# When the first inverse transform of a strip is placed: a planner's condition on VectorE's clock

## The chip, the cores and the metric

The kernel runs on one core of a Trainium2 chip. A core has TensorE (PE in the profile; its weight loads are shown apart as PEld), VectorE (DVE), ScalarE (ACT), GpSimd (POOL) and SyncE (SP, which here only issues transfers). Each engine works through its own list of instructions in order, and semaphores make it wait for other engines. The metric is the device time of one execution in microseconds (us), lower is better.

## The reference, cut to what matters

Four layers, each `x = x + layer(group_norm(x))`, on a float32 tensor of 4 images, 48 channels, 256 x 256 pixels. Only layer 0 is touched by the change:

```python
h = jnp.einsum('bchw,oc->bohw', x, w_in)                  # 48 -> 192 channels
h = jax.lax.conv_general_dilated(h, w_dw, ..., feature_group_count=2 * HID)   # 3x3, channel by channel
x1, x2 = jnp.split(h, 2, axis=1)
h = jax.nn.gelu(x1, approximate=False) * x2
y = jnp.einsum('bchw,oc->bohw', h, w_out)                 # 96 -> 48 channels
yp = y.reshape(b, c, Hp // P, P, Wp // P, P).transpose(0, 1, 2, 4, 3, 5)      # 8x8 blocks
f = jnp.fft.rfft2(yp.astype(jnp.float32)) * fft_w         # a mask on the block's spectrum
yp = jnp.fft.irfft2(f, s=(P, P))
```

Layers 1 and 2 are recurrent scans over rows and columns with small convolutions; layer 3 is like layer 0 with more channels and the transform in another place.

## The kernel before, in words

Layer 0 works through 64 strips, each of 8 rows of two images. For one strip n, the steps and their lines are these.

- `hidden` and `hidden_rest` (lines 278 to 296) make the 192 hidden channels by matmuls into PSUM tiles `ph`; ScalarE copies them into `main` (128 of the channels) and `rest` (64).
- Two generators `lane(0)` and `lane(1)` (line 300) do the 3x3 convolution of the main channels on TensorE: nine taps, each of 8 matmuls by a diagonal matrix (line 313), into a PSUM tile `pd`; one `yield` after each tap. Lane 0 ends in a gelu on ScalarE (`gl`, line 324), lane 1 in a product on VectorE (`g`, line 327). A lane waits at the start of an image until the strip's main half is `ready`.
- `unit` (line 334) does the convolution of the rest channels on VectorE, 16 instructions of line 352 a strip (`acc`), each about 1.3 us.
- `mixed` (lines 384 to 409) does the matmul back to 48 channels (`py`, lines 392 and 399) and a copy to `y`; `turned` (line 411) transposes it (`pt`, `yt`); `waves` (line 425) does the forward transform (`pf`, line 434), and VectorE multiplies with the mask in two instructions (`z`, line 438), one for each half.
- `back` (line 445) brings the strip back to pixels, in two pieces: `back(n, z, 0)` and `back(n, z, 8)`. Each does 32 matmuls (64 records in the profile) into a PSUM tile `po` (line 462), and eight additions of the input on VectorE (`xo`, line 473). The first piece reads the first half of `z` alone. The first issues the loads of `res` on SP (line 451); the second adds the statistics (line 482) and issues the stores on POOL (line 485).

All PSUM tiles of layer 0 share one pool, `ps`, with four buffers; a new tile waits until the engine that read the buffer's last tile is done.

The order is not left to a scheduler: `by_clocks` (line 565) writes it, while the program is built, with two planned clocks. `self.pe` is TensorE's: each step of a lane adds 0.54. `self.dve` is VectorE's. In each round both lanes take one step. Then pieces of `work()` (line 493) are placed, in their order. A piece is four things: a condition, a planned PE time, what it does, and a planned DVE time. It is placed when the credit that the lanes' steps have earned is not negative, when its condition holds, and, if it has a DVE time, when `self.dve` is less than 1.5 ahead of `self.pe`; its PE time is then taken from the credit, which grows to 2.0 at most. Lastly `due` (line 604) places VectorE's taps, as long as `self.dve` is not more than 1.0 ahead of `self.pe`. Placing the piece of `waves` moves `self.dve` by its planned 2.2 (`after`, line 600), so that right after it `self.dve` stands for the planned end of the mask. The condition of the first piece of `back` is `always`.

Of the kernel before, what the change touches and what calls it, by code (L numbers as in the profile page):

```python
# [33 lines left out]
class Net:  # L34
# [133 lines left out]
    def layer0(self, scs, stats):  # L168
# [7 lines left out]
        with ExitStack() as st:  # L176
# [11 lines left out]
            for half in range(2):  # L188
                lo = half * HID0
                for b in range(2):  # L190
                    s = slice(64 * b, 64 * b + C)
                    nc.sync.dma_start(wi[s, 64 * half : 64 * half + 64], self.a["L0_w_in"][:, lo : lo + 64])
                    at = 64 * half + 32 * b
# [16 lines left out]
            for j in range(4):  # L210
                s = slice(32 * j, 32 * j + 32)
                nc.sync.dma_start(wo[s, :, 0:C], self.a["L0_w_out"][0:64, :].rearrange("(k c) o -> c k o", c=32))
                at = 64 * (j % 2)
# [53 lines left out]
            def halo(n):  # L267
                h0 = strips[n][1]
                for z in (mains, rests):
                    new, old = z[n % 2], z[1 - n % 2]  # L270
                    if h0 == 0:
                        nc.gpsimd.memset(new[:, :, 0, 1 : W + 1], 0.0)
                    else:
                        nc.gpsimd.tensor_copy(new[:, :, 0:2, 1 : W + 1], old[:, :, RB : RB + 2, 1 : W + 1])
                    if h0 + RB == H:
                        nc.gpsimd.memset(new[:, :, RB + 1, 1 : W + 1], 0.0)
# [10 lines left out]
            def hidden_rest(n, xn, chunks):  # L287
                ph = sums("ph")
                for i, (r0, r1) in enumerate(chunks):
                    nc.tensor.matmul(  # L290
                        ph[:, i, 0 : r1 - r0, :], wi_r[0:112, :], xn[0:112, r0:r1, :], start=True, stop=True
                    )
                if all(r1 - r0 == R2 for r0, r1 in chunks):
                    chunks, ph = [(chunks[0][0], chunks[-1][1])], ph.rearrange("p i r w -> p (i r) w").unsqueeze(1)
                for i, (r0, r1) in enumerate(chunks):
                    nc.scalar.copy(rests[n % 2][:, 0, r0 + 1 : r1 + 1, 1 : W + 1], ph[:, i, 0 : r1 - r0, :])
# [148 lines left out]
            def back(n, z, q0):  # L445


                p, h0 = strips[n]
                res = sums_of[n % 2]
                for b in range(2 if q0 == 0 else 0):  # L450
                    nc.sync.dma_start(res[64 * b : 64 * b + C], self.x0[p, b * C : (b + 1) * C, h0 : h0 + RB, :])
                if q0 == 0:
                    state["xo"] = io.tile([CP, 2, self.WB, 2, RH, 2, 8], F32, name="xo", tag="xo")
                xo = state["xo"]
                for q0 in (q0,):
                    po = ps.tile([128, 2, 4, 2, 2, RH, 2, 4], F32, name="po", tag="w")
                    for q in range(4):
                        for l in range(2):
                            for lo, m in ((0, 64), (64, C)):
                                for o in range(2):  # L460
                                    f = slice(64 * o, 64 * o + 64)
                                    nc.tensor.matmul(
                                        po[lo : lo + m, o, q, :, :, :, l, :].rearrange("p e f h w -> p (e f h) w"),
                                        z[f, q0 // 2 + q, l, lo : lo + m], self.inv1_p[f, :],
                                        start=True, stop=True,
                                    )
                    rs = res[:, :, q0 * PW : (q0 + 8) * PW].rearrange(
                        "p (h e) (q w f) -> p e f q h w", e=2, f=2, q=8
                    )
                    for e in range(2):  # L470
                        for f in range(2):
                            for o in range(2):
                                nc.vector.tensor_tensor(
                                    xo[:, e, q0 // 2 : q0 // 2 + 4, f, :, o],
                                    po[0:CP, o, :, e, f].rearrange("p q h l w -> p q h (l w)"),
                                    rs[:, e, f, o::2], ALU.add,
                                )
                if q0 + 8 < NQ:
                    return
                flat = xo.rearrange("p e v f h l w -> p (e v f h l w)")  # L480
                for k in range(RB * W // MM):
                    nc.vector.bn_stats(stats[p][:, h0 * W // MM + k, :], flat[:, k * MM : (k + 1) * MM])
                to = self.strip(self.xs[0], p, h0 // 2, h0 // 2 + RH)
                for b in range(2):
                    nc.gpsimd.dma_start(
                        to[b].rearrange("c e v h w -> c (e v) (h w)"),
                        xo[64 * b : 64 * b + C].rearrange("p e v f h l w -> p (e v f) (h l w)"),
                    )

            ready, taken, state = set(), {}, {}  # L490
            full, until = {}, {}

            def work():


                always = lambda: True

                def enter(n):
                    return (lambda: n < 2 or taken.get(n - 2, 0) == 6), 0.0, lambda: halo(n), 0.0

                def fill(n, rest):
                    for k in range(0, 6 if strips[n][1] == 0 else 4, 2):
                        def go(k=k):
                            xn, chunks = state["xn"]
                            if rest:
                                hidden_rest(n, xn, chunks[k : k + 2])
                            else:
                                for r0, r1 in chunks[k : k + 2]:
                                    hidden(n, xn, r0, r1)
                            if k + 2 >= len(chunks):  # L510
                                ready.add((n, int(rest)))
                                if rest:
                                    full[n] = self.pe + 4.0
                        yield always, 1.8, go, 0.0

                early = self.norm_steps([stats[0]], self.grp7, "e", lambda name: sums(name)[0:CP, 0, 0, 0:1])

                parts_of = [1, 2, 2, 1]

                def advance():  # L520
                    try:
                        for _ in range(parts_of.pop(0)):
                            next(early)
                    except StopIteration as end:
                        state["first"] = self.by_image(0, end.value[0], nc.sync)

                fetch(0)
                fetch(1)
                state["xn"] = normed(0)
                yield enter(0)  # L530
                yield from fill(0, True)
                yield from fill(0, False)
                state["xn"] = normed(1)
                for n in range(len(strips) + 1):
                    if n == 4:
                        for which in ("down", "right", "left"):
                            self.scan_weights(1, which)
                    if n + 2 < len(strips):
                        fetch(n + 2)
                    if n > len(strips) // self.NP and "first" not in state:  # L540
                        yield always, 0.2, advance, 0.0
                    if n:
                        yield (
                            lambda: taken.get(n - 1, 0) == 6 and self.pe >= until[n - 1], 4.0,
                            lambda: state.update(y=mixed(n - 1)), 0.0,
                        )
                    if n + 1 < len(strips):
                        yield enter(n + 1)
                        yield from fill(n + 1, True)
                    if n:  # L550
                        yield always, 1.8, lambda: state.update(yt=turned(state["y"])), 0.0
                    if n + 1 < len(strips):
                        yield from fill(n + 1, False)
                    if n:
                        yield always, 1.7, lambda: state.update(z=waves(state["yt"])), 2.2
                    if n + 2 < len(strips):
                        state["xn"] = normed(n + 2)
                    if n:
                        yield always, 2.0, lambda: back(n - 1, state["z"], 0), 1.7
                        yield always, 1.1, lambda: back(n - 1, state["z"], 8), 4.4  # L560

            self.by_clocks([lane(0), lane(1)], work(), 0.54, [unit(n) for n in range(len(strips))])
            return state["first"]

# [1032 lines left out]
```

## Time and profile before

| | us |
|---|---|
| time before, median of 3 runs | 12764.71 (12756.09 to 12771.58) |
| the profiled execution | 12765.85 |
| its span, first to last instruction | 12764.0 |
| PE busy in the span | 11837.9 |
| DVE busy in the span | 7893.1 |
| ACT busy in the span | 4689.4 |

Layer 0's taps start at 259.4 us, and its last piece of `po` at 2968.5 us, so layer 0 is about a fifth of the span.

In a line of the profile that tells waits, "PE po L462 <- DVE z L438: 30.4, 26, 3.1" means that TensorE, ahead of an instruction of line 462 that writes `po`, waited for the instruction of line 438 on VectorE that writes `z`: 30.4 us in all, 26 times, 3.1 us the longest. "issue" is idle time in which the engine waited for nothing that the profile shows. In a line in order of time come the start, the duration, the engine, line, operation, tiles, shapes and the number of records; in brackets stands the idle time before it and who ended it. A float32 matmul shows as two records.

### The profile page before, as it was taken

The page shows a single profiled execution, that of the slowest core. Times are in us where ns is not written, and L with a number is a line of the kernel's source. Part 1 is how long each engine was busy: PE and PEld are TensorE (multiplying, and loading weights), DVE is VectorE, ACT ScalarE, POOL GpSimd, SP SyncE. Part 2 cuts the span into 40 slices and gives each one's busy share as a digit, 9 for nine tenths or more (in the row PEclk, how much of TensorE's full clock was granted, in tenths as well). Part 3 has the DMA queues.
Part 4 walks back from the last instruction along what each step waited for, and adds up shares of the span by engine and source line. Part 5 has one row for each costly group of instructions (what it writes and reads, how often), then busy time and mean ns, then how long its engine had stood idle before and what let it go on. Part 6 is the DMA issues. An engine that isn't in the chain of part 4 may idle for free. (4 is left out here: it accounts for less than half of the span.)

```text
span 12764.0 us, 411497 instructions
## 1 busy us (share of the span) xinstructions
PE 11837.9 (93%) x190576; PEld 7844.3 (61%) x190576; DVE 7893.1 (62%) x11132; ACT 4689.4 (37%) x5761; POOL 3135.4 (25%) x2017
## 2 busy tenths in 40 slices
PE   2999999999999999999999999989999999989998
PEld 1333333336777777777777777766666666666665
DVE  6777777774333334663333335668888777777787
ACT  1444444442223200002233000036666666666665
POOL 0000010000000001540000004534444444444344
PEclk9999999999999999999999999999999999999999
DMA  7222222226765876988756977931111111111110
GB/s 178 57 59 57 59 54 62 59 54 110 151 138 148 177 152 137 225 200 157 146 141 154 175 150 172 229 83 28 28 28 28 28 21 31 28 23 28 28 28 21
DMA packets 1170307, 1223.68 MB, mean 96 GB/s; under 512 B 1027668, under 2 KB 1031756, under 8 KB 1107724
## 3 DMA queue, kind: packets, MB, share of 16 engines
q1 hardware_dynamic: 1066052, 623.85, 26.6%
q0 software_dynamic: 87488, 445.55, 12.2%
q10 hardware_dynamic: 15048, 127.96, 5.4%
q8 instruction: 1494, 24.48, 0.8%
q14 instruction: 225, 1.84, 0.1%
HBM read 699.79 MB, written 497.42 MB: 94 GB/s over the span
## 5 line engine op out<-in xcount | busy, mean ns | idle before, releaser
L689 PE MATMUL acc<-line,w_down 96*96 96x256 f32 x12240 | 2660.9, 379 | 14.6 <-ACT line L787 4.9
L1269 POOL TENSOR_TENSOR acc_m<-acc_m,part 128x512 f32<-128x512 f32 (+1 forms) x1040 | 1820.0, 1771 | 2445.1 <-ACT part L1268 2423.7
L689 PEld LDWEIGHTS acc<-line,w_down 96*96 96x96 f32 x12240 | 1989.1, 163 | 671.7 <-DVE line L831 11.5
L1242 DVE SCALAR_TENSOR_TENSOR acc<-z_b,wd,acc 128x1024 f32<-128x1024 f32 (+1 forms) x1056 | 1818.3, 1722 | 40.9 <-ACT acc L1237 11.8
L313 PE MATMUL pd<-main,diag 32*32 32x512 f32 x36864 | 1401.8, 612 | 94.3 <-issue 54.9
L689 PE MATMUL acc<-line,w_right 96*96 96x256 f32 x6120 | 1339.6, 379 | 27.3 <-DVE line L869 22.1
L352 DVE SCALAR_TENSOR_TENSOR acc<-rest,wd,acc 128x1024 f32<-128x1024 f32 x1024 | 1275.2, 1303 | 145.0 <-ACT acc L344 144.8
L1178 PE MATMUL pd<-z_a,diag 32*32 32x512 f32 x37152 | 1317.7, 596 | 48.3 <-issue 43.2
L689 PE MATMUL acc<-line,w_left 96*96 96x256 f32 x6120 | 1336.6, 379 | 9.9 <-DVE line L910 7.5
L689 PEld LDWEIGHTS acc<-line,w_right 96*96 96x96 f32 x6120 | 997.0, 163 | 358.2 <-DVE line L869 22.9
L689 PEld LDWEIGHTS acc<-line,w_left 96*96 96x96 f32 x6120 | 994.7, 163 | 338.5 <-DVE line L910 16.4
L1178 PEld LDWEIGHTS pd<-z_a,diag 32*32 32x32 f32 x37152 | 793.9, 103 | 474.3 <-issue 196.3
L124 ACT ACTIVATE nrm<-nrm 96x2 f32<-96x2 f32 (+1 forms) x7 | 1.4, 203 | 2798.2 <-DVE nrm L123 2768.4
L872 DVE SCALAR_TENSOR_TENSOR line<-acc,b_right,in 96x256 f32<-96x256 f32 x1020 | 489.4, 480 | 850.7 <-PE acc L689 848.2
L796 DVE TENSOR_TENSOR line<-acc,in 96x256 f32<-96x256 f32 x1020 | 429.1, 421 | 920.0 <-PE acc L689 914.1
L831 DVE SCALAR_TENSOR_TENSOR line<-acc,b_down,in 96x256 f32<-96x256 f32 x992 | 476.0, 480 | 830.5 <-PE acc L689 821.9
L313 PEld LDWEIGHTS pd<-main,diag 32*32 32x32 f32 x36864 | 494.4, 104 | 780.2 <-issue 670.6
L1103 DVE TENSOR_TENSOR z<-pz,mask 128x768 f32<-128x768 f32 (+2 forms) x640 | 629.3, 1006 | 509.1 <-PE pz L1100 506.5
L920 POOL TENSOR_TENSOR blk<-blk,line 96x1024 f32<-96x1024 f32 x248 | 705.0, 2872 | 607.1 <-DVE line L910 607.1
L838 ACT COPY blk<-line 96x1024 f32<-96x1024 f32 (+2 forms) x264 | 480.0, 1891 | 921.8 <-DVE line L831 759.4
L910 DVE SCALAR_TENSOR_TENSOR line<-acc,b_left,in 96x256 f32<-96x256 f32 x992 | 475.6, 479 | 528.3 <-PE acc L689 528.3
L1268 ACT ACTIVATE part<-z_m,none,wd 128x512 f32<-128x512 f32 (+1 forms) x1040 | 786.1, 803 | 7.2 <-POOL acc_m L1269 7.1
(167 smaller groups left out, 13626.9 us busy)
## 6 DMA issues: line engine op xcount, KB each, us to landing
blk<-x ACTq DMA_DIRECT2D x64, 1536.0 KB, 17.5
in<-x SPq DMA_DIRECT2D x248, 384.0 KB, 11.1
dn<-line POOLq DMA_DIRECT2D x124, 768.0 KB, 9.8
rt<-line POOLq DMA_DIRECT2D x124, 768.0 KB, 9.9
in<-rt SPq DMA_DIRECT2D x124, 768.0 KB, 11.5
in<-dn SPq DMA_DIRECT2D x120, 768.0 KB, 6.5
in<-up SPq DMA_DIRECT2D x240, 384.0 KB, 11.5
up<-blk POOLq DMA_DIRECT2D x56, 1536.0 KB, 14.3
```

What stands on the lines that cost most here:

```text
L313: nc.tensor.matmul(pd[32 * j : 32 * j + 32, i], diag[s, t, :], z[s, R2 * j + t // 3 : R2 * j + t // 3 + R2, t % 3 : t % 3 + W], start=(t = ...
L352: nc.vector.scalar_tensor_tensor(to, at(t, r), wd[:, 1, t : t + 1], to, ALU.mult, ALU.add)
L689: self.nc.tensor.matmul(acc, w[:, t, :], carry[:, :, t : t + m], start=(t == 0), stop=(t == 2))
L831: nc.vector.scalar_tensor_tensor(inner(line), acc, bd, new[r], ALU.add, ALU.add)
L838: nc.scalar.copy(blk[:, :, e, lo:hi, k // 2 : k // 2 + RH], inner(ln[:, e::2])[..., lo:hi].rearrange("p h i w -> p i w h"),)
L872: nc.vector.scalar_tensor_tensor(blocks(inner(line)), blocks(acc), br, new, ALU.add, ALU.add)
L920: (nc.vector if w0 == 0 else nc.gpsimd).tensor_tensor(part, part, inner(ln[:, f::2])[..., lo:hi].rearrange("p w i h -> p i h w"), ALU.add)
L1103: nc.vector.tensor_tensor(zs[k][:, q0 : q0 + n].rearrange("p q b c -> p b q c"), pz[:, :, :, 0:NM], mask[:, :, :, NM * k : NM * k + NM].to ...
L1178: nc.tensor.matmul(pd[32 * j : 32 * j + 32, i, 0:n, :], diag[s, half, t, :], zt[g][s, R2 * j + t // 3 : R2 * j + t // 3 + n, t % 3 : t % 3 ...
L1242: nc.vector.scalar_tensor_tensor(acc, at(t), wd[:, half, t : t + 1], acc, ALU.mult, ALU.add)
L1268: nc.scalar.activation(part, half(at(t), r), AF.Identity, bias=none[0:n], scale=wd[0:n, 2, t : t + 1])
L1269: nc.gpsimd.tensor_tensor(half(acc, r), half(acc, r), part, ALU.add)
```

## The change

The first piece of `back` has a condition of its own. When it is first asked, it notes VectorE's planned time; the piece is placed only when TensorE's planned time has reached it. Before each strip's piece the noted time is cleared. The second piece keeps its condition.

```diff
                 always = lambda: True
+
+                def masked():
+                    if "at" not in state:
+                        state["at"] = self.dve
+                    return self.pe >= state["at"]
 
                 def enter(n):
...
                     if n:
-                        yield always, 2.0, lambda: back(n - 1, state["z"], 0), 1.7
+                        state.pop("at", None)
+                        yield masked, 2.0, lambda: back(n - 1, state["z"], 0), 1.7
                         yield always, 1.1, lambda: back(n - 1, state["z"], 8), 4.4
```

The condition is asked only when the credit isn't negative, and between `waves` and that moment `due` may have placed taps on VectorE, which also move its planned time.

## The prediction

> **What bounds the kernel now.** I read the page's head first: one core, and TensorE (PE) is busy almost throughout.
>
> ```profile
> span 12764.0 us, 411497 instructions
> PE 11837.9 (93%) x190576; PEld 7844.3 (61%) x190576; DVE 7893.1 (62%) x11132; ACT 4689.4 (37%) x5761; POOL 3135.4 (25%) x2017
> ```
>
> The change touches only layer 0, whose taps (`pd`, line 313) run from 259 us to about 2971 us. Over that stretch the windows give PE 2512 us of 2713 busy, VectorE (DVE) 2057, ScalarE (ACT) 1200: PE sets the pace and idles about 200 us. So the next view is the list of PE's own waits in that stretch (who it waited for, total, times, longest):
>
> ```profile
> PE pd L313 <- issue: 54.9, 35, 3.1
> PE po L462 <- issue: 35.1, 21, 3.4
> PE po L462 <- DVE z L438: 30.4, 26, 3.1
> PE ph L282 <- ACT main L285: 21.2, 21, 1.0
> PE pd L313 <- DVE z L438: 17.8, 11, 1.7
> PE pd L313 <- ACT gl L324: 17.8, 15, 2.1
> ```
>
> The product with the mask (`z`, line 438) holds PE up in two ways, which the change treats differently: 30.4 us at `po` (line 462), the piece that is moved, and 17.8 us at a new `pd`, which can't have its PSUM buffer before `z` has read `pf`. That 48.2 us is all there is to win by waiting more cleverly for the mask: 0.38%. A larger figure, 82.6 us of `po` weight loads waiting for `z`, should not be used; the weight-load row shows 0.84 us of idle at such places even when the matmul row shows none.
>
> Two strips in order of time show the two ways. First one where `po` waits:
>
> ```profile
> 1018.32 1.74 PE L434 MATMUL pf<-yt,c_fwd 64*64 64x448 f32 x16
> 1019.98 1.16 PE L313 MATMUL pd<-main,diag 32*32 32x512 f32 x32
> 1021.78 2.07 DVE L438 TENSOR_TENSOR z<-pf,mask 128x896 f32<-128x896 f32 x2
> 1022.91 1.15 PE L462 MATMUL po<-c_inv_p,z 64*64 64x64 f32 x64 [1.77 <-DVE z L438]
> 1024.14 1.68 DVE L473 TENSOR_TENSOR xo<-po,res 112x128 f32<-112x128 f32 x8 [0.29 <-PE po L462]
> ```
>
> `pf` ends at 1019.98, one round of taps (both lanes, 32 records) takes 1.09 us, and PE then stands 1.77 us: the first half of `z` (1.075 us of the 2.07) started late, behind taps of VectorE. `z`'s first half is thus ready about 2.85 us after `pf`, its second some 1.07 later. In the next strip the stall is at a new `pd`, and `po` behind it waits for nothing:
>
> ```profile
> 1060.87 1.16 PE L313 MATMUL pd<-main,diag 32*32 32x512 f32 x32
> 1063.66 1.15 PE L313 MATMUL pd<-main,diag 32*32 32x512 f32 x32 [1.63 <-DVE z L438]
> 1064.75 1.15 PE L462 MATMUL po<-c_inv_p,z 64*64 64x64 f32 x64
> ```
>
> **The change, part by part.** No instruction is added or removed; the order by clocks gives other positions. Comparing the order of instructions built from both codes:
>
> (a) *`po` comes one round later* in nearly every strip: after two or three rounds behind `pf` instead of one or two. Where it stalled 1.77 us, 1.77 - 1.09 = 0.68 us remains. In strips 0 to 29 the pattern repeats every five strips. Before, one cycle (strips 24 to 28) has 0.97 + 0.73, 0, 1.77, 1.63 and 0 = 5.1 us of waits for gelu and mask between `pf` and `po`. After: one strip with a new `pd` half a round later (1.63 - 0.54 = 1.09) and four with at most 0.68 = 3.8. Gain 1.3 us a cycle, six cycles: -8 us.
>
> (b) *What a saved stall gives back.* The rows "issue" total 92 us, waits for nothing the profile shows. They cut single pieces apart, such as this `po`, 9 records and then 55:
>
> ```profile
> 1617.85 0.38 PE L462 MATMUL po<-c_inv_p,z 64*64 64x64 f32 x9
> 1621.31 1.03 PE L462 MATMUL po<-c_inv_p,z 64*64 64x64 f32 x55 [3.08 <-issue]
> ```
>
> The Trainium skill ("Runtime: NRT & Kernel Launch", Instruction fetch mechanics) says that instructions stream in blocks of 256 and that this is mostly hidden, since issue is slower than the fetch. By that rule the -8 us is kept whole. The row speaks against it: a `po` is 64 matmuls and 64 weight loads in 1.08 us, and between `pf` and `py` the strips with a 1.65 or 1.77 us stall (11, 16, 21, 26, 38, 43, 48, 53, 58) have 0.9 us of issue gaps on average, those without one (13, 18, 23, 28, 40, 45, 50, 55, 60) have 2.4 us. That the gaps are fetching is not shown, but a stall there seems to be spent twice. The groups differ in their number of taps too, so I take half: +4 us, ends 0 and +8.
>
> (c) *The two tap lanes fall into step.* This the diff doesn't show. Before, lane 1 runs some rounds behind lane 0 in every strip, so `pd` tiles end one at a time. In the changed order lane 0 is held two steps near strip 30 (its main half isn't there yet), lane 1 catches up, and from strip 31 to the end both `pd` end and begin in the same round. PSUM has four such buffers (`ps`, 4), so two must come free at once, twice a strip.
> Between `pf` and `py`, per cycle of five (41 to 45): one strip where both new `pd` follow `pf` by one round and wait for both halves of `z` (1.66 + 0.5), two where `po` waits 0.68, one where two `po` are followed a round later by two new `pd` that wait for `xo` (eight adds, 1.68 us a `po`: 0.3 + 1.2), one with 0.3. Together 5.4 us against 5.1: +2 us over six and a half cycles.
> In mid-strip, where before almost nothing waits, there are three forms. 13 strips: a `ph` just before, whose copy ends 0.1 + 1.01 us after it while the first `pd` covers 0.54: 0.6 us. 8 strips: the gelu (1.03 us) is nearly covered: 0.2. 11 strips: both new `pd` follow `pt`, whose two copies take 1.71 us (0.15 + 0.5), and the second `ph` then waits for the gate product (1.03 gelu, then 1.215 us product, up to one 1.3 us tap before it: 0 to 0.7): 1.0. Sum 7.8 + 1.6 + 11 = +20 us; ends 0 (the copies come earlier than I place them) and +45 (a VectorE tap ahead of every product).
> The skill ("Perfetto Trace Analysis", Optimization Strategy) says that a gap that repeats on the saturated engine can mean that there isn't enough PSUM for the next tile. It would charge more for this than the rows do: an unhidden gelu and product, 2.2 us, at each of 65 joint ends is 145 us. I take the rows, since the two free buffers cover most of it.
>
> (d) *VectorE does one or two more taps between `z` and `xo`* (1.28 us each), and while `po` 0 waits the order saves up credit, so in 26 strips `po` 8 follows at once. Two buffers are then held until two sets of adds (3.4 us) are done. Five of the 26 are in (c). In the others the next new tile comes two rounds later (2.2 us) or one; I take 0.6 us for each of 21: +12 us, ends 0 and 1.7 x 21 = 36.
> The output DMA waits for `xo` on POOL, and the next `res` load on SP: both move by one tap, 1.3 us. POOL's wait for `xo` is already 707 us, and `res` is needed a strip (42 us) later; landing takes 6 to 8 us. Nothing for these, and 1.3 us a strip if that slack were gone.
> ACT has 1513 us idle in the stretch; its moved gelus count only as in (c). Behind a waiting `po` or `pd` all PE work of the strip queues, and then `y`, `rest` and `main` on ACT: they go late by the stall itself, not again.
>
> Sum: -8 + 4 + 2 + 20 + 12 = +30 us on the profiled execution's 12765.85 us (span 12764.0 and 1.85 around it): 12795.9. The median of the runs is 1.1 us under the profiled one: **12794 us**, +0.23%. What measurement of this kernel can tell from no change is about 0.2%, 25.5 us.
>
> **The rivals.**
> *Hidden or given back.* The issue gaps swallow (a) whole, and the staggered first half shows that two free buffers suffice: (c) and (d) bring 5 us or so. Time about 12768. For it: one cycle of five strips takes 206 us (975.32 to 1181.70) and the one ahead of it (758.05 to 975.32) 217 us before the change, with the same order, so gaps of this kind move more time than the mask does. Against it: (c) is a lasting change of structure in 33 strips.
> *Faster.* The mask's 48.2 us and part of the gelu's 17.8 go, and joint ends are free because ACT is idle over half the time. Less the remainders of 0.68 in some 30 strips (20 us): -45, about 12720 to 12735. It decides if joint ends cost less than 0.5 us a strip and gaps give nothing back. Against it: 11 of the 37 mask waits stand at `pd`, where moving `po` does nothing.
> *Much slower.* Every pair of adjoining `po` holds two of four buffers through a late set of adds, 1.68 us and more in 26 strips, and every joint end pays a tap in front of the product: +36 and +45 on top of (a): about +75, 12840. For it: the adds follow one tap more than before. Against it: `py` waits for `xo` only 2.0 us in all now.
> *Nothing happens* is excluded: the built order differs in nearly every strip.
>
> **How the numbers follow.** The forecast (own range 12765 to 12830) has 0.50, hidden 0.17, faster 0.21, much slower 0.12. The range leaves out the outer part of faster and of much slower, a tenth at each side: 12733 to 12847. Slower by over 0.2% (above 12790.2): 0.6 of the forecast and all of much slower = 0.42. Within 0.2%: the rest of the forecast and nearly all of hidden, 0.36. Faster: 0.22.
>
> **What would show it.** In the list of PE's waits after the change: `po` for `z` down from 30.4 to under 20 us (a); issue rows over 92 us (b); new rows of `pd` for `rest`, `yt`, `gl`, `z` and `xo` after about 1610 us, and the stretch from there to layer 0's end longer than the 1361 us of before while the first half is no longer (c); `pd` or `py` waiting for `xo` well over 2.0 us (d). The rest of the kernel should keep its length. I am wrong if lanes in step cost PE nothing, or if PE's waits fall and the time with them.

## The result, and the profile after

The changed kernel takes 12789.27 us (median of 17 runs, 12768.46 to 12827.14), the kernel before 12773.54 us in the same comparison (17 runs, 12756.09 to 12797.55). The ratio is 1.0014, with a 95% interval of 1.0007 to 1.0020: slower by some 18 us, clear of noise, and smaller than the 0.2% (25.5 us) that the prediction gave as what measurement can tell from no change. The forecast was 12794 us, 1.0023.

The head of the page of the changed kernel: TensorE (PE) has the same instructions and 20 us more busy time.

```profile
span 12784.7 us, 411481 instructions
PE 11858.4 (93%) x190576; PEld 7860.0 (61%) x190576; DVE 7877.3 (62%) x11132; ACT 4692.7 (37%) x5761; POOL 3166.9 (25%) x2017
```

From the list of PE's own waits in layer 0 of the changed kernel, the rows that bear on the parts of the prediction:

```profile
PE po L462 <- issue: 41.6, 22, 3.8
PE pd L313 <- issue: 39.6, 27, 3.1
PE pd L313 <- ACT gl L324: 21.9, 14, 2.1
PE pd L313 <- DVE z L438: 15.0, 12, 1.9
PE po L462 <- DVE z L438: 12.8, 11, 1.9
PE ph L282 <- ACT gl L324: 11.7, 11, 1.2
PE po L462 <- DVE xo L473: 3.4, 8, 0.4
PE pd L313 <- ACT yt L420: 2.5, 11, 0.2
PE py L392 <- DVE xo L473: 2.0, 5, 0.6
```

The condition did what it says: `po` waits 12.8 us for the mask instead of 30.4, and a new `pd` 15.0 instead of 17.8. The row of `ph` for `gl` grew from one wait to eleven, each a little over one microsecond. Two windows of 30 strips show where the time is: strips 0 to 29 (first `pf` to the `pf` of strip 30), then 30 to 59. First the kernel before, then the changed one; the columns are the length and the busy time of PE, its weight loads, DVE, ACT and POOL, then the granted clock, the DMA share and the GB/s that the DMA engines moved.

```profile
321.00:1609.80 1288.80, 1190.01 (x24075) 483.72 (x24070) 967.69 (x1266) 563.88 (x546) 117.46 (x122) 0.97 0.27 57
1609.80:2873.00 1263.20, 1173.16 (x23908) 476.04 (x23908) 965.61 (x1270) 564.85 (x543) 124.72 (x121) 0.98 0.27 58
```
```profile
326.90:1596.20 1269.30, 1179.88 (x24142) 484.48 (x24138) 967.04 (x1268) 565.59 (x547) 134.36 (x123) 0.99 0.27 58
1596.20:2894.20 1298.00, 1205.17 (x23812) 487.49 (x23812) 958.57 (x1267) 566.10 (x542) 132.06 (x120) 0.97 0.27 56
```

The half in which the lanes are apart became 19.5 us shorter, the half in which they run in step 34.8 us longer. In the second half PE's busy time grew by 32 us for the same work. The traces show two reasons.

One is the granted clock, 0.97 and 0.98 in the two halves before, 0.99 and 0.97 after. In layer 0 of these traces it is either 1.0 or 0.5, and 0.5 for 3.4 us or a few times that. In the first half these stretches add up to 65 us before and 35 us after, in the second to 44 and 71 us. At most half of such a stretch is lost, so up to 15 of the 19.5 us and up to 13 of the 34.8 us are clock. The stretches follow idle time. All of them start on one grid of 3.413 us. In layer 0, in the 3.4 us ahead of each of the 28 starts before and the 26 after, the matmul row is idle for 1.18 us or more. Not every such span is followed by one: of the 32 before with 1.7 us or more of idle time, 26 are. But after the 704 and 709 spans with less than 1 us, none starts. So a stall can be paid a second time, and the prediction has no term for that.

The other reason is stalls that the matmul row hides. A matmul of `pd` is recorded as 0.59 us long, though one starts every 0.034 us, so a stall shorter than about 0.55 us leaves no idle time in PE's row: it lies under the tail of the matmuls before it. The weight-load row shows such stalls, though its sums are not lost time: a place can stand there with 0.84 us without any stall, as the prediction says. Four rows of the changed kernel, from 1596 to 2894 us:

```profile
PEld ph L282 <- ACT gl L324: 20.4, 11, 2.0
PEld pd L313 <- ACT rest L296: 11.9, 12, 1.0
PEld pd L313 <- ACT yt L420: 11.7, 22, 0.6
PEld ph L282 <- DVE g L327: 10.4, 11, 1.0
```

None of these four rows is in that list of the kernel before in its second half. They name what new tiles wait for at the joint ends of the lanes: the gelu, the copies `rest` and `yt`, the product `g`.

### The profile page after: what moved, and what is told of

Same layout as the page of the kernel before. It is cut to its first block, busy times and chain, and to the rows that moved or that the text cites. A ratio compares the mean times of both kernels' runs of the same rounds, so it can differ in the third digit from the quotient of the medians.

```text
span 12784.7 us, 411481 instructions
## 1 busy us (share of the span) xinstructions
PE 11858.4 (93%) x190576; PEld 7860.0 (61%) x190576; DVE 7877.3 (62%) x11132; ACT 4692.7 (37%) x5761; POOL 3166.9 (25%) x2017
## 3 DMA queue, kind: packets, MB, share of 16 engines
q8 instruction: 1494, 24.48, 0.8%
## 5 line engine op out<-in xcount | busy, mean ns | idle before, releaser
L695 PEld LDWEIGHTS acc<-line,w_down 96*96 96x96 f32 x12240 | 1989.0, 163 | 671.7 <-DVE line L837 11.5
L313 PE MATMUL pd<-main,diag 32*32 32x512 f32 x36864 | 1429.2, 611 | 85.1 <-issue 39.6
L695 PE MATMUL acc<-line,w_right 96*96 96x256 f32 x6120 | 1338.7, 379 | 24.7 <-DVE line L875 19.5
```

Source lines behind the costliest of these rows:

```text
L313: nc.tensor.matmul(pd[32 * j : 32 * j + 32, i], diag[s, t, :], z[s, R2 * j + t // 3 : R2 * j + t // 3 + R2, t % 3 : t % 3 + W], start=(t = ...
L695: self.nc.tensor.matmul(acc, w[:, t, :], carry[:, :, t : t + m], start=(t == 0), stop=(t == 2))
```

## The experiments

"Lag" is the distance, in rounds, by which lane 1 starts an image behind lane 0, counted in the built order. In the kernel before it is 4.5 in the first strips and 2.5 from strip 5 to the end; in the changed kernel the same up to strip 31, and from strip 32, one later than the prediction has it, 0.5: both lanes begin in the same round, in step. Ratios are to the kernel before, timed on the same chip in the same session, with 95% intervals.

### The wait without the lanes in step, and the lanes in step without the wait

**e1_wait_30**: the wait in 30 strips only.

```diff
-                        yield masked, 2.0, lambda: back(n - 1, state["z"], 0), 1.7
+                        yield (masked if n < 30 else always), 2.0, lambda: back(n - 1, state["z"], 0), 1.7
```

> The changed kernel, but the condition on the mask holds only while n < 30; from then on the first piece back is placed as before, and the two tap lanes never fall into step. Theory (the wait alone gains, the lanes in step cost): faster than before by 5 to 20 us, about 12755 to 12768, with the second half of layer 0 as long as before. Rival 1 (issue gaps swallow every saved stall): within 5 us of before. Rival 2 (late additions after adjoining po pieces are the cost): slower than before by 5 to 15 us.

Measured: 0.9981 (0.9973 to 0.9990), 24 us faster by the ratio. That looks like the theory, but it is not clean. In the built order lane 0 is held one step near strip 32, and from there the lag is 1.5 instead of 2.5; the run e7 below shows that this alone is worth something.

**e2_step_31**: the kernel before, lane 0 waiting once.

```diff
                         while (n, 0) not in ready:
                             yield False
+                        while l == 0 and n == 31 and state["t1"] < 31 * 18:
+                            yield False
...
+                            if l == 1:
+                                state["t1"] = 18 * n + 9 * img + t + 1
                             yield True
```

> The kernel before, without the wait for the mask; lane 0 only waits once, at strip 31, until lane 1 has come level, so the lanes are in step from there on, as in the changed kernel. Theory: slower than before by 20 to 45 us, all of it after 1600 us. Rival 1: within 5 us of before. Rival 2: within 5 us of before, since no po pieces adjoin.

Measured: 1.0035 (1.0021 to 1.0048), 45 us slower, at the upper end of what I expected. Lanes in step cost, without any wait for the mask.

**e4_step_all**: the kernel before, both lanes starting together.

```diff
-                if k == 1 and count < 4:
+                if k == 1 and count < 0:
```

> The kernel before, without the wait; both lanes start together, so they are in step in all 64 strips. Theory: slower than before by about twice what lanes in step from strip 31 cost, 40 to 90 us, 12815 to 12865. Rival 1 and rival 2: within 5 us of before.

Measured: 1.0048 (1.0033 to 1.0062), 61 us. Slower again, by less than twice the 45.

**e3_wait_apart**: the wait in all strips, lane 1 held at least four taps behind.

```diff
-                if k == 1 and count < 4:
+                if k == 1 and steps[0] - steps[1] < 4:
                     continue
...
+                steps[k] += bool(got)
```

> The changed kernel with the wait in all 64 strips, but lane 1 is kept at least four taps behind lane 0, so the lanes never fall into step. Theory: faster than before by 10 to 40 us, about 12735 to 12765. Rival 1: within 5 us of before. Rival 2: slower than before by 10 to 25 us.

Measured: 1.0009 (1.0000 to 1.0019), at best no change. The theory expected a gain and was wrong. This edit also makes the lag 3.5, so I separated the two.

### The lag by itself, and the wait at the lag of before

**e5_wait_lag_2** is e3 with `< 3`: lag 2.5 throughout.

> The changed kernel with the wait in all strips, and lane 1 held so that it starts each image 2.5 rounds after lane 0 throughout, which is the distance that the kernel before has in nearly all strips (the run with four taps had 3.5). Theory (the wait gains, and the run before this one lost by the other distance): faster than before by 15 to 40 us, about twice the gain of the run with the wait in 30 strips. Rival (the wait gains nothing by itself in all strips): within 10 us of before.

**e6_apart_only** is e3's edit in the kernel before (lag 3.5, no wait), and **e7_lag_1** the same with `< 2` (lag 1.5, no wait).

> The kernel before, without the wait; lane 1 starts each image 3.5 rounds after lane 0 instead of 2.5. Theory (the distance itself costs): slower than before by 15 to 40 us. Rival (the distance is free, and the wait in all strips was what cost in the run with both): within 10 us of before.

> The kernel before, without the wait; lane 1 starts each image 1.5 rounds after lane 0 instead of 2.5. Theory (only a joint end, two buffers at once, costs much): within 15 us of before. Rival (any distance other than 2.5 costs): slower by 20 us or more.

**e9_wait_lag_1** is the changed kernel with `< 2`: wait, lag 1.5.

> The changed kernel with the wait in all strips, and lane 1 1.5 rounds behind lane 0 throughout, the distance that was fastest without the wait (0.9985). Theory (what the wait saves is given back in issue gaps): within 10 us of that kernel, about 0.998 to 0.9995 of before. Rival (the wait gains at this distance): 0.997 or less.

| lag | without the wait | with the wait |
|---|---|---|
| 3.5 | 1.0027 (1.0015 to 1.0038) | 1.0009 (1.0000 to 1.0019) |
| 2.5 | 1 (the kernel before) | 1.0008 (0.9999 to 1.0017) |
| 1.5 | 0.9985 (0.9976 to 0.9993) | 1.0010 (1.0001 to 1.0018) |
| 0.5 in the second half | 1.0035 (1.0021 to 1.0048), e2 | 1.0014 (1.0007 to 1.0020), the changed kernel |

So the wait gains in step and, with intervals that just overlap, at 3.5; it loses at 1.5, and does nothing that can be told at 2.5. With lanes apart at the lag of before, "the wait gains by itself" has fallen. The lag matters as much as the wait, and not only because of joint ends: 3.5 costs 0.27%. Of what was expected, the rival held for e5 and the theory for e6; e7 was faster than either had it, and e9 missed both.

PE's waits show where the rows at 2.5 and 1.5 come from. With the wait at lag 2.5 (e5):

```profile
PE pd L313 <- issue: 68.8, 37, 3.3
PE po L462 <- issue: 55.4, 27, 4.3
PE pd L313 <- ACT gl L324: 36.9, 24, 2.1
PE pd L313 <- DVE z L438: 7.9, 11, 0.7
PE po L462 <- DVE z L438: 0.5, 1, 0.5
```

The mask's 48.2 us have come down to 8.4, which leaves little more for this change to reach. In their place the two issue rows of `pd` and `po` went from 90 to 124 us and the wait for the gelu from 17.8 to 36.9. That is 53 us more, in place of the 40 saved. At lag 1.5 with the wait (e9) the mask is back, at the other place:

```profile
PE pd L313 <- DVE z L438: 57.5, 23, 3.3
```

In the built order a new `pd` now falls between `pf` and `po` in 39 of 64 strips, against 15 without the wait (e7). It has to wait for `z` to free a PSUM buffer, so a later `po` does not help.

The granted clock takes part here too. Each run has its mean clock on record, and the span times (1 - clock) is at most what that run lost by it. The differences of the means to the kernel before in the same session, in us (the clock is recorded in steps of 0.001, 12.8 us, so single runs are coarse):

| run | runs | time | of it at most the clock |
|---|---|---|---|
| e5, wait, lag 2.5 | 13 | +14 | +20 |
| e9, wait, lag 1.5 | 13 | +9 | +24 |
| e7, lag 1.5 | 11 | -17 | +3 |
| e3, wait, lag 3.5 | 14 | +12 | -3 |
| e6, lag 3.5 | 9 | +34 | +19 |
| e2, in step from strip 31 | 6 | +45 | +13 |
| e4, in step in all strips | 6 | +62 | +15 |

For e5 and e9 the clock can account for the whole loss: by this estimate the wait at lag 2.5 would be some 6 us faster than before at an equal clock, no more than its noise. The gain of the wait at 3.5 can be all clock. The lanes in step cost 32 us or more that the clock can't account for. For the changed kernel's 18 us I can't do this sum, since its comparison has no clock on record for the runs of before.

**e8_mask_early** goes at the same stall from VectorE's side, in the kernel before:

```diff
-                while k not in begun or self.dve > self.pe + 1.0 or self.pe < begun[k]:
+                while k not in begun or self.dve > self.pe + self.ahead or self.pe < begun[k]:
...
                     if n:
+                        self.ahead = -0.5
                         yield always, 1.7, lambda: state.update(z=waves(state["yt"])), 2.2
+                        self.ahead = 1.0
```

> The kernel before, without the wait; instead VectorE's taps are held back while the forward transform is the next piece (planned VectorE time at most 0.5 behind TensorE's instead of 1.0 ahead), so that the mask is computed sooner. All positions of TensorE's pieces are nearly as before. Theory (the stall at po and pd is VectorE's taps ahead of the mask): the waits for z fall from 48 to under 25 us, and the time by 10 to 25 us. Rival (a saved stall is given back in issue gaps): the waits for z fall, the issue rows grow by as much, and the time stays within 5 us.

Measured: 1.0025 (1.0016 to 1.0034), slower, which neither had expected. PE's waits in layer 0:

```profile
PE pd L313 <- issue: 90.6, 49, 3.9
PE po L462 <- issue: 36.0, 18, 3.6
PE pd L313 <- ACT gl L324: 35.1, 16, 3.5
PE pd L313 <- DVE z L438: 16.7, 10, 1.7
PE pd L313 <- ACT main L285: 14.4, 12, 1.2
PE ph L282 <- ACT main L285: 1.0, 1, 1.0
PE po L462 <- DVE z L438: 0.9, 2, 0.5
```

The waits for the mask fell from 48.2 to 17.6 us, as both had it. The two issue rows grew from 90 to 127 us, as the rival said, and the wait of `pd` for the gelu by 17. The waits for `main` only moved: 12 us more at `pd`, 20 less at `ph`. The clock can account for up to 28 of the 34 us between the means. Why the gelu's row rises no run isolates.

### What the issue rows are

In the kernel before I counted PE's records (matmuls, weight loads, queue entries) up to each cut of over 0.9 us that falls inside a run of one line. Of 68 such cuts 53 stand at the same place modulo 256. The Trainium skill ("Runtime: NRT & Kernel Launch", Instruction fetch mechanics) says that instructions are fetched in blocks of 256; the count agrees. It also says that this is mostly hidden, and here it is not. The kernel before's page lists these transfers:

```profile
q8 instruction: 1494, 24.48, 0.8%
```

That is 1494 packets of 16 KiB, one for each 256 of TensorE's 382,552 records. In layer 0 there are 45 stretches of over 0.9 us, inside the work on one tile, in which neither a matmul nor a weight load runs. Of these 44 end 1.2 to 1.7 us after such a packet has landed, and at one and the same place modulo 256; of moments taken at random 9% fall so. In the changed kernel it is 35 of 36. If the blocks come late because of other transfers, taking those away must close the gaps. Three kernels leave out layer 0's loads of the input and the residual after the second strip:

```diff
-                for b in range(2):
+                for b in range(2 if n < 2 else 0):
                     nc.sync.dma_start(
                         raw[64 * b : 64 * b + C, ...
...
-                for b in range(2 if q0 == 0 else 0):
+                for b in range(2 if q0 == 0 and n < 2 else 0):
                     nc.sync.dma_start(res[...
```

> The kernel before, leaving out layer 0's loads of the input and of the residual after the second strip (both stay in their buffers from strips 0 and 1), which takes away about 96 of the 156 MB moved in layer 0; order and work of all engines as before. Theory (the issue gaps are instruction blocks fetched beside that traffic): the issue rows fall from 93 us to under 50, and the time by 20 us or more. Rival (the fetch is slow by itself, or the gaps are something else): the issue rows and the time stay within 10 us.

> The kernel with the wait in all strips and lane 1 2.5 rounds behind, leaving out the same loads. Theory (the saved stall was given back in issue gaps, and with the traffic gone it is kept): 10 to 35 us faster than the kernel before with the same loads left out. Rival (the wait costs by itself): no faster than that kernel, and if the issue rows did not fall there, as much slower as with the loads, about 10 us.

> The changed kernel, leaving out the same loads. Theory: lanes in step from strip 31 still cost 20 to 45 us and the wait now gains 10 to 35, so within 25 us of the kernel before with the same loads left out, and slower than the kernel with the wait and the lanes apart by 20 us or more. Rival: the same distance to the kernel before as with the loads, 18 us slower.

| with the loads left out | median us | the four runs | strips 0-29, 30-59 |
|---|---|---|---|
| kernel before (r1) | 12627.99 | 12607.36 to 12637.83 | 1212.7, 1206.6 |
| wait, lag 2.5 (r2) | 12616.53 | 12607.02 to 12622.65 | 1202.3, 1206.1 |
| changed kernel (r3) | 12700.58 | 12673.97 to 12706.96 | 1210.0, 1257.2 |

The kernel before falls to 0.9865 (0.9851 to 0.9878). Its PE waits then:

```profile
PE po L462 <- DVE z L438: 30.2, 26, 3.1
PE ph L282 <- ACT main L285: 21.2, 21, 1.0
PE pd L313 <- ACT gl L324: 17.8, 15, 2.1
PE pd L313 <- DVE z L438: 17.8, 11, 1.7
PE pd L313 <- issue: 1.7, 1, 1.7
```

The four waits on other engines are what they were, to 0.2 us. `po` has no issue row left among those listed, and `pd` has 1.7 us of its 54.9. That the issue rows are instruction blocks that come late is shown: the gaps stand at block boundaries, they end when a block has landed, and they go when 97 MB of loads go. How the loads delay a block is not: the packets in layer 0 took 1.05 us with them and 1.04 without, in the median.

The time fell by 168 us between the medians, and by 133 between the two profiled executions (the runs of before that r1 is compared with were slower than its profiled execution). The two windows of layer 0 alone are 132.7 us shorter: 88 are the issue rows, up to 29 more are clock, which was at 0.5 for 109 us of these windows before and for 51 without the loads. The rest, some 15 us, is not accounted for.

With the gaps gone the wait at lag 2.5 is 11.5 us faster in the medians, the direction the theory gave; the ranges of the four runs overlap, so it is not clear of noise. The lanes in step now cost more, not the same: the changed kernel is 73 us above the kernel before, all four runs above all four. The theory had this within 25 us and the rival at 18, both wrong; the theory was right that it is over 20 us above the wait at lag 2.5. Its second half by window, the kernel before and then the changed one, both without the loads:

```profile
1539.50:2746.10 1206.60, 1153.70 (x23912) 475.43 (x23915) 963.83 (x1270) 564.93 (x543) 125.52 (x121) 0.99 0.13 22
```
```profile
1536.60:2793.80 1257.20, 1192.76 (x23813) 482.00 (x23813) 961.94 (x1268) 567.38 (x542) 132.91 (x120) 0.98 0.12 21
```

The second half in step is 50.6 us longer without the gaps, and 34.8 with them, up to 12 and 13 us of it clock. A stall in front of a late block could take time that the block would have taken anyway, which would make the second figure smaller. This is not shown: in the profile of e2, with the gaps, that half is 40.4 us longer than before. The first half with the wait is 2.7 us shorter (r3), or 10.4 with the lag of e5 (r2), with up to 8.5 and 6.8 us less lost by the clock, so no gain of the wait itself can be read from the lengths.

The other 25 us of the 73 are no stalls of the lanes. Most of them lie in layer 3, where no instruction moved: it takes 4337.5 us at a granted clock of 0.98 in r1 and 4359.0 at 0.97 in r3, and the time at half clock there is 48 us longer, of which half is 24. So they can all be clock. Why the clock differs there is open.

## Why the prediction was right, and which of its terms were not

**(a) The mask's stall.** Right in its place: `po` was to fall under 20 us and is 12.8. The size of its gain, 8 us in 30 strips, isn't shown. Without the loads, PE's waits in the first half are 53.2 us before and 48.5 after, 5 us less, and the lengths differ by 2.7 us with clock in them. The 19.5 us of the first half in the one profile of the changed kernel are mostly clock, and kernels with the same order in that half differ by more than 9 us (1288.8 and 1298.5 in the kernel before and e2, 1269.3 and 1278.5 in the changed one and e1).

**(b) What a saved stall gives back.** I took half and named the price of the fetch an open matter. With the lanes at the lag of before nothing is left of the saving in time (e5: 40 us of waits saved, 34 us more in issue rows, 19 more for the gelu, and the clock lower by up to 20 us). My sign for the changed kernel was wrong: its two issue rows did not rise above 90 us, they are 81. The rule that the fetch is hidden was rightly not followed. What I read as a stall "spent twice" has a second form that I left out: the half clock behind idle time.

**(c) Lanes in step.** This decided the sign, as forecast, and was the term mis-sized. I had +22 us; without the wait it is 45 (e2), and without gaps 50.6 (r3 against r1, with the wait's gain already in it). The failing step is the third form of mid-strip end, where both new `pd` follow `pt`. I had put the gelu directly behind the two copies `yt`, done 2.0 us after `pt`. In the order of the changed kernel two instructions of the rest channels stand between:

```profile
2232.73 1.75 PE L416 MATMUL pt<-c_ident,y 112*128 112x112 f32 x16
2233.76 1.71 ACT L420 COPY yt<-pt 128x896 f32<-128x896 f32 x2 [2.18 <-PE pt L416]
2234.72 3.02 PE L313 MATMUL pd<-main,diag 32*32 32x512 f32 x64 [0.23 <-ACT yt L420]
2235.36 1.25 ACT L344 ACTIVATE acc<-rest,none,wd 128x1024 f32<-128x1024 f32 x1
2236.63 1.05 ACT L361 ACTIVATE gr<-acc 64x1024 f32<-64x1024 f32 x1
2237.71 1.02 ACT L324 ACTIVATE gl<-pd 128x1024 f32<-128x1024 f32 x1
2238.77 1.22 DVE L327 TENSOR_TENSOR g<-gl,pd 128x1024 f32<-128x1024 f32 x1 [7.35 <-ACT gl L324]
2238.79 2.70 PE L282 MATMUL ph<-xn,wi 48*128 48x512 f32 x8 [1.05 <-ACT gl L324]
2241.42 2.01 PE L313 MATMUL pd<-main,diag 32*32 32x512 f32 x32
```

The gelu starts at 2237.71, not about 2235.5, so `ph` waits 1.05 us for it. The two rounds of `pd` ahead of it take 3.02 us instead of 2.35, with a wait of 0.23 in front. The 2.70 us of `ph` and the 2.01 us of the next round, which takes 1.14 otherwise, are not all stall: the granted clock is 0.5 from 2240.70 on.

```profile
2232.73:2240.70 7.97, 6.56 (x93) 3.16 (x88) 1.93 (x2) 6.61 (x7) 0.00 (x0) 1.00 0.01 2
2240.70:2244.10 3.40, 3.40 (x38) 0.78 (x36) 1.71 (x2) 2.83 (x4) 0.00 (x0) 0.50 0.00 0
```

The same form at full clock, in an earlier strip, shows the stall alone:

```profile
1932.81 2.38 PE L282 MATMUL ph<-xn,wi 48*128 48x512 f32 x8 [1.05 <-ACT gl L324]
1935.12 1.14 PE L313 MATMUL pd<-main,diag 32*32 32x512 f32 x32
```

Its `ph` takes 2.38 us instead of 2.04, since the second tile waits for the product, and the next round takes its usual time. That is 0.23 + 0.67 + 1.05 + 0.34 = 2.3 us in a strip that I had at 1.0. Eleven strips of this form, 1.3 us more each, are 14 us. The clock, for which I had put nothing, can have cost the second half 12 to 17 us more with the lanes in step than without (13 in the changed kernel, 17 in e2, 12 in r3 against r1). Together that is about the 23 to 28 missing. The rule on too little PSUM, at 145 us, would have been far too high.

**(d) Late additions and adjoining pieces.** Too high, as far as the matmul row shows: waits for `xo` are 5.4 us in the rows above, against 2.0 before, where I took 12. That stores and loads on POOL and SP cost nothing fits: no row of PE names them.

So the path was right, lanes that fall into step in a half that the diff doesn't name, and the number was in part luck: +30 was near the measured 18 with terms wrong in opposite directions, (c) half of what was measured, (d) and the +4 of (b) too high, and the clock at nothing. How the 45 us of e2 become 18 with the wait is not taken apart by any run. Of the rivals, "given back" was right that issue gaps can swallow a saving and wrong that nothing would be lost. "Faster" fails on e5, where the mask's waits do go and the time stays. "Much slower" fails on the waits for `xo`.

## What to carry to other kernels

Where a planner writes the order, a condition on one piece can shift the phase of others; compare the whole built order to its end, since here the cost began in strip 32 and came from lanes that the edit doesn't name. A stall that is taken away is worth its length only if nothing next in line is late by itself: when idle time "for nothing" returns at multiples of a fixed number of instructions, the instruction stream is such a thing. And before a window's length is put down to waits, compare its granted clock: here up to 15 us of a difference of 19.5 were clock. Of the kernels here the lag of 1.5 without the wait (0.9985) is the simplest that beats both; the wait in 30 strips with that lag after them (0.9981) can't be told from it.

## What the runs showed of the hardware that I had not expected

Of some 400 instruction blocks that TensorE fetched in layer 0, one in seven left an idle row "issue", some 90 us of layer 0's 2713, at a DMA share of only 0.27; at 0.12 nearly none did. The four largest waits for other engines, taken with and without this traffic, agree to 0.2 us, so they are fixed by the order; the gaps are what varies.

The clock went to 0.5 for 3.4 us behind spans of 3.4 us with 1.18 us or more of idle time on TensorE, 28 times in layer 0 before; a round of `pd` under it took 2.01 us instead of 1.14 in the changed kernel. Between orders with the same work and the same loads, the mean clock differed by up to 28 us of a run (e8 against before).
